# Reordering the pieces of a causal attention layer around its first and last tiles

## The chip, the cores and the metric

The kernel runs on one core of one Trainium2 chip. The metric is the device time of one execution in microseconds (us), lower is better; a number given for several runs is their median.

## The reference

An image of 256 channels and 64 x 64 positions goes through two layers in float32. Layer 0 is a convolution-like linear attention over windows, with its result added to the image. For layer 1 the image is 4096 tokens of 256 values; `t` below is the token matrix. It has two halves:

```
def causal(x):                      # x = layer norm of t, 4096 x 256
    q, k, v = x Wq + bq, x Wk + bk, x Wv + bv
    A = q k^T                       # 4096 x 4096, one head
    A = where(causal, A, MASK_FILL) / 16
    out = layernorm(softmax(A) v + x) * g_ln + beta_ln
    h = relu(out W1 + b1) W2 + b2
    return layernorm(h) * g_lnff + beta_lnff
t = t + causal(layernorm(t))
t = t + experts(layernorm(t))       # 2 of 8 experts, the same for all tokens
```

The routing of the experts needs the mean of the normalised tokens over all 4096 positions, so that no expert product can start before the last token has passed the causal half.

## The kernel before

`conv_attn_hybrid` builds one program of three stages: `window_attention` (layer 0), `causal_attention` and `experts`. This document is about `causal_attention`.

The 4096 tokens are 32 tiles of 128, in eight groups of four (group g holds tiles 4g to 4g + 3). A tile's scores are its queries against all keys up to its own position. Tiles 12 to 31 (`BIG` is 12) are called large, tiles 0 to 11 small. Large tiles are worked from 31 down to 12 in the list `larges`, small tiles from 0 up to 11 in `smalls`. One round of the main loop takes the large tile i and, as long as there are any, a small one.

The steps of a tile are these, with the names and lines that the profile shows:

- `queries(g)` (L950, L952): four matrix products of 512 columns for a group's queries, evicted by ScalarE (ACT) into `qT`.
- `scores(i)` gives a list of parts of 512 keys each. A part is two products into PSUM buffer `pa` (L991), an eviction by ACT into the row buffer `s` (large) or `ss` (small) (L993), for the first part a mask on GpSimd (POOL) (L996), and a maximum on VectorE (DVE) (L999). The last part also gives the row's maximum (L1002, L1003) and starts the exponential over the whole row on ACT (L1004).
- `attend(i)` gives a list of steps. `turn` transposes four blocks of 128 columns into PSUM buffer `pt` (L1021), and DVE copies them into `sT` (L1024, L1026 for the short block behind the row). `add` multiplies them with the values into `po` (L1035). The block behind the row carries the masked positions together; its product is with `after`. A step is the transposition of the next four blocks and then the products of these four. After the last step `finish` divides and takes statistics (L1045, L1047, L731, L732).
- `layers(g, j0, j1)` is what follows when a group's tiles are finished: six pieces `first` (normalise, L1075), `turn` (L1083, L1084), `hidden` (W1, L1092, L1094), `last` (W2 for four tiles, L1102, L1104, then L1109 and L1110), `norm` (L1117), `turn_again` (L1125 and L1126, whose result is the experts' input). The pieces wait in the list `later`; the main loop takes one at a time with `one()`. Group 3, the last to be finished, goes in two parts: tiles 1 to 3 of it when three are done, tile 0 at the end.
- `causal.values(g)` (L889, L891) gives four tiles of values.

PSUM buffers `pa`, `pt`, `po` and `pm` have two copies each, `sT` three. Only TensorE's (PE's) order is written out by hand, as the code calls it (`tc.manual_schedule`). The instructions of the other engines are placed by the framework's scheduler; each engine then works through its own list in order, and a wait at its head holds all behind it.

At the start of the stage, values and scores alternate: tile 31 is scored in eight parts, with `causal.values(6)`, `(5)` and `(4)` after the first three parts and `behind()` (which makes `after`) after the fifth. Small tile 0's queries and scores come in the first round.

Of the kernel before, what the change touches and what calls it, by code (L numbers as in the profile page):

```python
# [11 lines left out]
F32 = mybir.dt.float32  # L12
# [7 lines left out]
P = 128  # L20
# [707 lines left out]
def statistics(nc, pool, src, mv):  # L728

    st = pool.tile([P, 6], F32, name="lnst", bufs=4)  # L730
    nc.vector.bn_stats(out=st, in_=src)  # L731
    nc.vector.bn_aggr(out=mv, in_=st)  # L732


def rsqrt(nc, var, eps):
    nc.scalar.activation(var, var, AF.Sqrt, bias=eps)
    nc.vector.reciprocal(var, var)


BIG = NT - 20  # L740
# [184 lines left out]
def causal_attention(tc, t, ident, eps5, causal, big, given):  # L925
# [3 lines left out]
    nc = tc.nc  # L929
    with ExitStack() as ctx:  # L930
# [77 lines left out]
        def attend(i):  # L1008
# [5 lines left out]
            g = i // 4  # L1014
# [24 lines left out]
            def finish(acc):  # L1039
                if g not in atts:  # L1040
                    atts[g] = (sm.tile([P, 4, D], F32, name="att", bufs=3), sm.tile([P, 4, 2], F32, name="mvs", bufs=3), [])
                att, mvs, done = atts[g]
                xn = normalised(nc, sm, t[:, i, :], stats[:, i, 0:1], stats[:, i, 1:2], "xn", 2)
                l = sm.tile([P, 1], F32, name="l")
                nc.vector.reciprocal(l, acc[:, 0:1])  # L1045
                aj = att[:, i - 4 * g, :]
                nc.vector.scalar_tensor_tensor(aj, acc[:, 1:], l, xn, op0=ALU.mult, op1=ALU.add)  # L1047
                statistics(nc, sm, aj, mvs[:, i - 4 * g, :])
                done.append(i)
                if 4 * g != BIG:  # L1050
                    if len(done) == 4:
                        later.extend(layers(g, 0, 4))
                elif len(done) == 3:
                    later.extend(layers(g, 1, 4))
                elif len(done) == 4:
                    later.extend(layers(g, 0, 1))

            def step(at):
                if at + 1 < len(groups):
# [5 lines left out]
        def layers(g, j0, j1):  # L1065

            att, mvs, _ = atts[g]
            js, width, tail = range(j0, j1), (j1 - j0) * P, 4 * g == BIG
            state = {}

            def first():
# [21 lines left out]
                                         rhs=state["aT"][:, c, 0:width], start=(c == 0), stop=(c == DC - 1))  # L1093
                    nc.scalar.activation(hT[:, e, 0:width], pp[:, 0:width], AF.Relu, bias=col["b1"][:, e : e + 1])  # L1094

            def last():
                y, hT = att, state["hT"]
                mvy = sm.tile([P, 4, 2], F32, name="mvy")
                for j in js:
                    py = ps.tile([P, 512], F32, name="pm")  # L1100
                    for c in range(DC):
                        nc.tensor.matmul(py[:, 0:D], lhsT=hT[:, c, (j - j0) * P : (j - j0 + 1) * P], rhs=wt["W2"][:, c, :],  # L1102
                                         start=(c == 0), stop=(c == DC - 1))
                    nc.vector.tensor_add(y[:, j, :], py[:, 0:D], row["b2"])  # L1104
                    statistics(nc, sm, y[:, j, :], mvy[:, j, :])
                rsqrt(nc, mvy[:, j0:j1, 1], eps5)
                for j in js:
                    yj, tj = y[:, j, :], t[:, 4 * g + j, :]
                    nc.vector.scalar_tensor_tensor(yj, yj, mvy[:, j, 0:1], row["g_lnff"], op0=ALU.subtract, op1=ALU.mult)  # L1109
                    nc.vector.scalar_tensor_tensor(tj, yj, mvy[:, j, 1:2], tj, op0=ALU.mult, op1=ALU.add)  # L1110
                    statistics(nc, sm, tj, given.stats[:, 4 * g + j, :])

            def norm():
                rsqrt(nc, given.stats[:, 4 * g + j0 : 4 * g + j1, 1], eps5)
                for j in js:
                    s = given.stats[:, 4 * g + j, :]
                    nc.vector.tensor_scalar(att[:, j, :].rearrange("p (c q) -> p c q", c=DC),  # L1117
                                            t[:, 4 * g + j, :].rearrange("p (q c) -> p c q", c=DC),
                                            s[:, 0:1], s[:, 1:2], op0=ALU.subtract, op1=ALU.mult)
# [7 lines left out]
                                         accum_out=given.sums[:, c, given.parts : given.parts + 1])  # L1127
                given.parts += 1

            return [first, turn, hidden, last, norm, turn_again]  # L1130

        later = []
        with tc.manual_schedule(engines={mybir.EngineType.PE}):
# [9 lines left out]
            def one():  # L1143
                if later:
                    later.pop(0)()
# [1 line left out]
            causal.values(3, value_psum)  # L1147
            need(larges[0])
            causal.values(7, value_psum)
            for at, part in enumerate(scores(larges[0])):  # L1150
                part()
                if at < 3:
                    causal.values(6 - at, value_psum)
                if at == 4:
                    behind()
            for r, i in enumerate(larges):
                small = smalls.pop(0) if smalls else None
                if small is not None:
# [5 lines left out]
                if r + 1 < len(larges):  # L1164
# [4 lines left out]
                    one()  # L1169
                    todo.pop(0)()  # L1170
                    parts[-1]()
                if r == len(larges) - 1:
                    while todo:
                        todo.pop(0)()
                        one()
                half = len(todo) // 2
                for step in todo[:half]:
                    step()
                one()
                for step in todo[half:]:  # L1180
                    step()
                if small is not None:
                    for step in attend(small):
                        step()
                one()
            while later:
                one()
# [177 lines left out]
```

## Time and profile before

| | us |
|---|---|
| median of three runs | 1963.89 |
| lowest, highest | 1961.94, 1965.53 |
| the profiled execution's own time | 1963.31 |
| its span, first to last instruction | 1961.6 |
| mean granted TensorE clock | 0.988 of full |
| PE busy | 1867.7 (95%) |
| DVE busy | 1013.5 (52%) |
| ACT busy | 780.3 (40%) |
| POOL busy | 438.8 (22%) |

The causal stage lies between about 998 and 1717 us of the span; layer 0 lies before it, the routing from 1718 and the experts' products from 1730 to the end. In a row of the timeline the first number is the start in us from the span's start, the second the duration, and what stands in square brackets at the end is the idle time of the engine before this instruction and the instruction whose end released it.

### The profile page before, as it was taken

What the parts mean: (1) busy time and instruction counts of PE and PEld (TensorE: products, weight loads), DVE (VectorE), ACT (ScalarE), POOL (GpSimd) and SP (SyncE); (2) the same over time, 40 slices, a digit from 0 to 9 for tenths busy, and PEclk for the clock granted to TensorE, in tenths of its full rate; (3) what the DMA queues carried; (4) which work ended last, traced back from release to release, by engine and by line L of the source; (5) the groups of instructions that cost most, each with busy time, mean ns of one, the idle gap of its engine ahead of it and who ended that gap; (6) DMA issues with size and microseconds to landing.
All of it is one profiled execution on the core that took longest, in us unless ns stands there. A gap on an engine that the chain in (4) does not pass through costs nothing.

```text
span 1961.6 us, 50126 instructions
## 1 busy us (share of the span) xinstructions
PE 1867.7 (95%) x22286; PEld 1272.9 (65%) x22286; DVE 1013.5 (52%) x2154; ACT 780.3 (40%) x1295; POOL 438.8 (22%) x709
## 2 busy tenths in 40 slices
PE   3999999999999999999999999999999999789998
PEld 2666666666566667666665666665666666557777
DVE  4644555564654466666653435454554555543343
ACT  0566544444456645444413333233332333223322
POOL 1286233342255133432100000000000000031120
PEclk9999999999999999999999999999999999879999
DMA  8211100000331100002000000000000000010000
GB/s 246 75 56 41 40 14 14 19 19 13 112 88 37 49 19 19 13 13 51 13 2 1 0 1 0 1 1 1 0 1 0 1 1 1 1 43 22 22 22 22
DMA packets 66905, 53.58 MB, mean 27 GB/s; under 512 B 37568, under 2 KB 56792, under 8 KB 66688
## 3 DMA queue, kind: packets, MB, share of 16 engines
q1 hardware_dynamic: 57296, 31.87, 6.0%
q10 hardware_dynamic: 8128, 14.67, 2.1%
q0 software_dynamic: 1264, 3.84, 0.6%
q8 instruction: 174, 2.85, 0.6%
q14 instruction: 43, 0.35, 0.1%
HBM read 32.93 MB, written 17.44 MB: 26 GB/s over the span
## 4 chain that ended last, share of the span: by engine, by line
PE 43%; DVE 6%; ACT 3%; issue 1%; POOL 0%; ACTq 0%; DVEq 0%; POOLq 0%
PE po L1035 12%; PE pa L991 10%; PE ph L1299 6%; PE py L1319 6%; PE pt L1021 2%; PE pm L1092 1%; PE acc L395 1%; PE pm L1102 1%; PE ps L362 1%; PE ps L507 1%; DVE sT L1024 1%; DVE nbs L999 1%; DVE lnst L731 1%; PE pm L950 1%; ACT s L1004 1%
## 5 line engine op out<-in xcount | busy, mean ns | idle before, releaser
L330 ACT ACTIVATE pm<-ps 128x512 f32<-128x512 f32 (+24 forms) x690 | 358.4, 584 | 330.6 <-PE ps L362 176.8
L332 DVE TENSOR_SCALAR pm<-ps 128x512 f32<-128x512 f32 (+21 forms) x414 | 265.3, 668 | 265.2 <-PE ps L362 172.7
L362 PE MATMUL ps<-q,kh 32*128 32x217 f32 (+27 forms) x3872 | 213.1, 336 | 0.0
L395 PE MATMUL acc<-pm,vh 128*32 128x217 f32 (+27 forms) x3872 | 199.7, 329 | 0.0
L991 PE MATMUL pa<-k,qT 128*128 128x512 f32 (+3 forms) x416 | 180.2, 574 | 7.1 <-ACT qT L952 5.7
L362 PEld LDWEIGHTS ps<-q,kh 32*128 32x128 f32 x3872 | 161.2, 185 | 9.7
L1024 DVE COPY sT<-pt 128x512 f32<-128x512 f32 (+3 forms) x144 | 92.5, 642 | 143.1 <-PE pt L1021 142.9
L353 PE MATMUL ps<-table,table 32*128 32x184 bf16 (+36 forms) x2904 | 142.7, 245 | 5.4 <-issue 1.2
L395 PEld LDWEIGHTS acc<-pm,vh 128*32 128x32 f32 x3872 | 98.0, 109 | 71.7 <-issue 37.1
L430 POOL TENSOR_TENSOR y<-y,rn 128x512 f32<-128x512 f32 x32 | 40.9, 1277 | 432.8 <-DVE y L429 358.2
L993 ACT ACTIVATE s<-pa,v 128x512 f32<-128x512 f32 (+3 forms) x112 | 73.8, 661 | 152.2 <-PE pa L991 152.1
L991 PEld LDWEIGHTS pa<-k,qT 128*128 128x128 f32 x416 | 75.7, 191 | 89.3 <-issue 72.4
L353 PEld LDWEIGHTS <-table 32*128 32x128 bf16 x2904 | 57.0, 92 | 108.4 <-issue 97.6
L999 DVE TENSOR_REDUCE nbs<-s 128x1 f32<-128x512 f32 (+4 forms) x120 | 77.5, 651 | 80.6 <-ACT s L993 59.2
L1319 PE MATMUL py<-w,hT 128*128 128x256 f32 x512 | 111.8, 379 | 0.0
L1035 PE MATMUL po<-kh,sT 128*128 128x257 f32 x406 | 102.9, 395 | 8.7 <-DVE sT L1024 8.5
L1319 PEld LDWEIGHTS py<-w,hT 128*128 128x128 f32 x512 | 97.3, 190 | 15.7 <-issue 1.9
L362 PE MATMUL ps<-q,k 32*128 32x192 f32 (+30 forms) x1936 | 102.8, 337 | 0.0
L395 PE MATMUL acc<-pm,v 128*32 128x192 f32 (+30 forms) x1936 | 95.9, 326 | 0.6 <-issue 0.6
L507 PE MATMUL ps<-l0wo,y 128*128 128x256 f32 x384 | 90.7, 387 | 0.0
L1035 PEld LDWEIGHTS po<-kh,sT 128*128 128x128 f32 x406 | 74.7, 195 | 22.3 <-DVE sT L1024 12.7
L982 POOL MEMSET s<- 128x32 f32 x20 | 2.5, 124 | 376.5 <-PE pt L1021 348.4
(305 smaller groups left out, 2997.0 us busy)
## 6 DMA issues: line engine op xcount, KB each, us to landing
oscratch<-ov ACTq DMA_DIRECT2D x32, 256.0 KB
ov<-oscratch SPq DMA_DIRECT2D x32, 256.0 KB
t<-in_xT SPq DMA_DIRECT2D x32, 128.0 KB
vscratch<-v SPq DMA_DIRECT2D x32, 128.0 KB
vh<-vscratch SPq DMA_DIRECT2D x16, 256.0 KB
raw<-in_x ACTq DMA_DIRECT2D x7, 512.0 KB
raw<-in_x SPq DMA_DIRECT2D x7, 512.0 KB
out<-y SPq DMA_DIRECT2D x7, 512.0 KB
```

The source lines that it names most:

```text
L330: nc.scalar.activation(dst, src, AF.Relu)
L332: nc.vector.tensor_scalar_max(dst, src, 0.0)
L353: nc.tensor.matmul(got[h][:, spot].rearrange("p (y x) -> p y x", y=part.r1 - part.r0), lhsT=spread[hs, int(part.vertical), :], rhs=bias[hs ...
L362: nc.tensor.matmul(got[h][:, spot].rearrange("p (y x) -> p y x", y=part.r1 - part.r0), lhsT=keys[hs], rhs=q[hs, part.r0 : part.r1, part.c0 ...
L395: nc.tensor.matmul(out, lhsT=v, rhs=pm[:, h, spot].rearrange("p (y x) -> p y x", y=part.r1 - part.r0), start=fresh, stop=(left[key] == 0), ...
L507: nc.tensor.matmul(pt[:, i * D : (i + 1) * D], lhsT=ys[wi, Y][:, (2 * j + i) * P : (2 * j + i + 1) * P], rhs=wo[:, n, :], start=(n == 0), ...
L991: nc.tensor.matmul(pp[:, 0:m], lhsT=qTs[g][:, c, i * P - g * 512 : n - g * 512], rhs=x[b // 512][c][:, 0:m], start=(c == 0), stop=(c == DC ...
L999: nc.vector.tensor_reduce(nbs[:, at : at + 1], s[:, b : b + m], AX.X, ALU.max)
L1024: nc.vector.tensor_copy(sT[:, 0:full], pt[:, 0:full])
L1035: nc.tensor.matmul(acc, lhsT=sT[0:m, j * P : (j + 1) * P], rhs=rhs, start=(b == 0), stop=(m != P))
L1299: nc.tensor.matmul(ph, lhsT=w1v[:, e, c, f, :], rhs=x2[g][c], start=(c == 0), stop=(c == DC - 1))
L1319: nc.tensor.matmul(py, lhsT=hT[:, e, f, j * P : (j + 1) * P], rhs=w2v[:, e, f, :], start=(e + f == 0), stop=(e == 1 and f == FC - 1))
```

## The change

The change is in `layers`, in `finish` and in the main loop.

- At the start, the parts of tile 31's scores follow each other without values between them. After six of the eight parts come the queries and scores of small tile 0; then the last two parts, then the values of groups 4, 5 and 6, then small tile 0's attention. The small tiles thereby run one round ahead, and the round of tile 20 no longer has one.
- In a round, the small tile's first transposition is issued before the large tile's last step, and its other steps after it.
- A `layers` list of four tiles has nine pieces: `last` is two pieces of two tiles, and the scaling (L1109, L1110 and statistics) is a step `scale` of its own, also in two pieces. The square root of the last statistics moves from `norm` to the end of `scale`.
- `one()` is called at a third and two thirds of a large tile's steps, where it was called at the half.
- The last group goes as tiles 2 and 3, then tiles 0 and 1.

In the changed kernel the line numbers behind line 1053 differ: L1075, L1083, L1084, L1092, L1094, L1109, L1110, L1117, L1125, L1126 become L1073, L1081, L1082, L1090, L1092, L1113, L1114, L1122, L1130, L1131. The lines for queries, scores and attention, L1102 and L1104 stay. No computation is added or removed.

```diff
-                elif len(done) == 3:
-                    later.extend(layers(g, 1, 4))
-                elif len(done) == 4:
-                    later.extend(layers(g, 0, 1))
+                elif len(done) % 2 == 0:
+                    later.extend(layers(g, 4 - len(done), 6 - len(done)))
...
-            def last():
+            def last(sub):
                 y, hT = att, state["hT"]
-                mvy = sm.tile([P, 4, 2], F32, name="mvy")
-                for j in js:
+                if sub[0] == j0:
+                    state["mvy"] = sm.tile([P, 4, 2], F32, name="mvy")
+                mvy = state["mvy"]
+                for j in sub:
...
-                rsqrt(nc, mvy[:, j0:j1, 1], eps5)
-                for j in js:
+                if sub[-1] == j1 - 1:
+                    rsqrt(nc, mvy[:, j0:j1, 1], eps5)
+
+            def scale(sub):
+                y, mvy = att, state["mvy"]
+                for j in sub:
                     yj, tj = y[:, j, :], t[:, 4 * g + j, :]
                     nc.vector.scalar_tensor_tensor(yj, yj, mvy[:, j, 0:1], row["g_lnff"], op0=ALU.subtract, op1=ALU.mult)
                     nc.vector.scalar_tensor_tensor(tj, yj, mvy[:, j, 1:2], tj, op0=ALU.mult, op1=ALU.add)
                     statistics(nc, sm, tj, given.stats[:, 4 * g + j, :])
+                if sub[-1] == j1 - 1:
+                    rsqrt(nc, given.stats[:, 4 * g + j0 : 4 * g + j1, 1], eps5)
 
             def norm():
-                rsqrt(nc, given.stats[:, 4 * g + j0 : 4 * g + j1, 1], eps5)
...
-            return [first, turn, hidden, last, norm, turn_again]
+            subs = [(j, j + 1) for j in range(j0, j1, 2)]
+            return ([first, turn, hidden] + [lambda sub=sub: last(sub) for sub in subs]
+                    + [lambda sub=sub: scale(sub) for sub in subs] + [norm, turn_again])
...
-            for at, part in enumerate(scores(larges[0])):
-                part()
-                if at < 3:
-                    causal.values(6 - at, value_psum)
-                if at == 4:
+            for at, large in enumerate(scores(larges[0])):
+                large()
+                if at == 3:
                     behind()
+                if at == 5:
+                    need(smalls[0])
+                    first = smalls.pop(0)
+                    for part in scores(first):
+                        part()
+            for g in (4, 5, 6):
+                causal.values(g, value_psum)
+            for step in attend(first):
+                step()
...
-                if r == len(larges) - 1:
-                    while todo:
-                        todo.pop(0)()
+                behind_it = attend(small) if small is not None else []
+                pauses = range(len(todo)) if r == len(larges) - 1 else (len(todo) // 3, 2 * len(todo) // 3)
+                for at, step in enumerate(todo):
+                    if at == len(todo) - 1 and behind_it:
+                        behind_it.pop(0)()
+                    step()
+                    if at in pauses:
                         one()
-                half = len(todo) // 2
-                for step in todo[:half]:
+                for step in behind_it:
                     step()
-                one()
-                for step in todo[half:]:
-                    step()
-                if small is not None:
-                    for step in attend(small):
-                        step()
                 one()
```

## The prediction

> **What bounds the kernel now.** I read the page's first part first, then the chain, then the causal layer alone (about 1000 to 1718 us, all that the diff touches): its waits on PE, its stretches with the granted clock, and the timeline at each long wait.
>
> ```profile
> PE 1867.7 (95%) x22286; PEld 1272.9 (65%) x22286; DVE 1013.5 (52%) x2154; ACT 780.3 (40%) x1295; POOL 438.8 (22%) x709
> PE 43%; DVE 6%; ACT 3%; issue 1%; POOL 0%; ACTq 0%; DVEq 0%; POOLq 0%
> ```
>
> TensorE is the bound. The change adds no matrix work, so it can only give back time in which PE waits or runs at half clock. The waits of PE in the layer (total, times, longest):
>
> ```profile
> PE po L1035 <- DVE sT L1024: 8.5, 15, 1.5
> PE pt L1125 <- DVE att L1117: 7.5, 2, 4.0
> PE pa L991 <- ACT qT L952: 6.7, 6, 4.2
> PE pt L1021 <- ACT kh L1126: 3.8, 2, 2.1
> PE pt L1021 <- DVE aT L1084: 3.0, 5, 1.1
> PE pt L1083 <- DVE att L1075: 2.4, 1, 2.4
> PE po L1035 <- DVE sT L1026: 1.9, 2, 1.0
> PE pt L1021 <- ACT v L1126: 1.5, 3, 0.8
> ```
>
> Together 35 us. The true loss of a wait is some 0.16 us more than the idle shown: a transposition shows 0.27 us but back to back they start 0.11 apart. Now the stretches (columns: us, then busy PE, PEld, DVE, ACT, POOL, granted clock):
>
> ```profile
> 1035.95:1040.10 4.15, 0.00 (x0) 0.00 (x0) 0.00 (x0) 4.15 (x3) 0.00 (x0) 0.92 0.00 0
> 1040.10:1046.20 6.10, 6.10 (x11) 3.46 (x12) 1.21 (x4) 1.90 (x4) 0.58 (x2) 0.50 0.01 1
> 1226.00:1230.50 4.50, 2.78 (x14) 1.71 (x13) 3.98 (x17) 0.30 (x1) 0.22 (x2) 1.00 0.00 0
> 1230.60:1234.00 3.40, 3.40 (x9) 2.25 (x7) 1.42 (x5) 0.00 (x0) 0.64 (x1) 0.50 0.02 5
> 1686.00:1691.30 5.30, 5.17 (x16) 4.12 (x16) 2.01 (x3) 0.00 (x0) 0.00 (x0) 0.50 0.01 3
> 1702.05:1718.23 16.18, 7.09 (x23) 4.61 (x23) 10.09 (x36) 4.64 (x15) 1.51 (x3) 0.70 0.00 0
> ```
>
> Each longer hole is followed by a stretch at clock 0.50, which costs half its length again. The timeline says who held PE:
>
> ```profile
> 1035.74 3.73 ACT L1004 ACTIVATE s<-s,nb 128x4128 f32<-128x4128 f32 x1
> 1039.38 1.25 ACT L952 ACTIVATE qT<-pm,ik 128x512 f32<-128x512 f32 x2
> 1040.10 1.38 PE L991 MATMUL pa<-k,qT 128*128 128x128 f32 x4 [4.15 <-ACT qT L952]
> 1076.35 0.70 PE L1035 MATMUL po<-kh,sT 128*128 128x257 f32 x2 [0.61 <-DVE sT L1024]
> 1227.75 0.69 PE L1035 MATMUL po<-after,sT 32*128 32x257 f32 x2 [0.96 <-DVE sT L1026]
> 1656.71 2.01 PE L1035 MATMUL po<-kh,sT 128*128 128x257 f32 x8 [1.49 <-DVE sT L1024]
> ```
>
> **The change part by part.** Numbers are sums against the profiled execution's own 1963.31 us (span 1961.6 and 1.7 around it), 0.6 below the median of the three runs.
>
> *First exponentials under values.* Before, tile 31's exponential (table load 1.28 and 3.73 us) stands on ACT ahead of the evictions of the queries for small tile 0: PE idles 4.15 us, then 6.1 us at half clock lose 3.05. After, these queries and small 0's scores come before the last two score parts, and values 4, 5, 6 (12 tiles of 0.87 us, 10.4 us) follow, with small 0's attention. The large exponential ends some 6 us after the last part (eviction and reduction 0.69 each, 3.73, hops), under the 10.4. What comes in its place is the wait for a qT eviction as at the group boundary at 1189.49, 0.56 shown (0.7 in true loss); behind it on PE stand small 0's score and the two last parts, all now earlier than before. VectorE's value additions (0.42 each) keep PE's pace; three short waits on them, 0.2 to 0.5 us, stay about as they are. Gain 4.3 + 3.05 − 0.7 = 6.7.
>
> *Small transpositions ahead of the large tile's last step.* Twelve hand-overs between small transposition and product wait 0.35 to 0.76 us shown, 6.1 together, 8.0 in true loss. Small 0 keeps its own (0.77): nothing stands behind it. The cover of the others is the large tile's last step: zero to three products of 0.44 and one with `after` of 0.44. Needed are hop, copy (0.28 to 0.69) and hop, near 0.9. For tiles 31, 27 and 23 the last step has only the `after` product, so 0.2 to 0.4 stays; for tile 28 the second half of a `last` (L1104) comes just before, some 0.5 stays. Left over 2.0; gain 6.0. The change moves no DMA, and SP's queue keeps its order; POOL's memsets, masks and additions (0.1 to 0.64 each) move with the pieces and small scores by up to a round, on an engine that idles up to 30 us between them.
>
> *Layers in nine pieces.* The large `after` product at 1227.75 (and one at 1393.76, 0.97) stood behind a whole `last`: four L1104, four L1109, four L1110 and eight statistics, some 8 us of VectorE. In halves, and with the pieces that fall there (`first`, `turn`) behind other steps, these waits go: 1.9 + 0.3; with them the reason for the half clock at 1230.6 to 1234, 1.7. Gain 3.9. If the copies stay late, this is zero.
>
> The waits of transpositions for a pt buffer (3.0 on aT, 5.3 on L1126) depend on what a piece precedes. Counting pops (five a round with a small tile, four without): `turn` stands before another transposition only for tiles 20, 18, 15 and, with half width, 13; `turn_again` for tiles 27, 25, 23, 21 and 16, none of them just behind a large exponential. The others stand before scores. At 0.3 to 0.5 each, 3.5 of 8.3 stays: gain 4.8. In the late rounds (tiles 19 to 13) copies still queue behind layer steps on VectorE, as at 1656.71. Adding up that place again, from the start of the second half of `last`: VectorE has to the first copy's end two L1104 (0.84), five statistics and six aggregates (3.1), four L1109 (1.8), two L1110 (0.9), three score reductions (1.75), the tile's finish and small ones (1.2) and the copy (0.69), 10.3, of which 0.5 lies ahead: 9.8. PE has 1.74, scores of 0.87 and three of 1.72, and two turns, 8.6: a wait of 1.2 for 1.49. I count zero.
>
> *Table switches.* Sqrt and Exp alternate 14 times instead of 12: 28 loads for 24.
>
> ```profile
> L1004 ACT ACT_TABLE_LOAD x12 | 15.4, 1283 | 19.7 <-DVE nb L1003 19.7
> ```
>
> Four more are 5.1 us of ACT, of which the layer uses some 35%. The Trainium skill ("ScalarE: Activation LUTs", What ACT_TABLE_LOAD costs) speaks against it: a switch is 2.66 us, load and drain, so 10.6 us. In the trace the exponential at 1035.74 starts 0.02 after its load's end, and I take 1.28. They cost PE something only before an eviction it needs; such score waits are 0.2 to 0.6 before and about as many after: zero. Without the cover of two pa buffers, 5.1.
>
> *Last group by pairs.* Before, the last round (1682.17 to 1702.05) holds 14.3 us of products, 2.6 of waiting for L1075 and 3.0 of half clock; then 16.2 to the router's first product at 1718.23. After, the first pair's layer is over but for its scaling; the two rounds' products are 2 us fewer before the end of attention. But `turn_again` comes two steps (4.4 us) after `scale`, whose chain on VectorE (two L1109, two L1110, statistics, two Sqrt with hops, two L1117) takes some 7 with the copies in between: a new wait near 2.3. Behind it on PE stand tile 12's last transposition and its last six products, and everything after waits for those. So 0.2 to 3.6 us is gained there, by whether the clock falls. Behind it two tiles go through the chain: 0.4 more at each of five steps, 2 us more of products at half clock, less 2.5 for what the end before lost behind the first three tiles (L1110 to 1703.45, L1117, pt). Together −1.5 to +4.5; I take +1.
>
> The clock once more. The Trainium skill ("TensorE: Matmul & The Clock Gate", Part 1: The HAM clock gate) halves the clock after an idle window of about 3.4 us and restores it after a busy one. By that the first hole would cost 1.7, and the two of under 1 us at 1227 and 1230 none; the trace gave 3.05 and 1.7. By the rule the sum is 3 us less. I take the trace; for the end the rule speaks against pairs, and is in the sum.
>
> Sum: 6.7 + 6.0 + 3.9 + 4.8 + 1 = 22.4. I take 1.4 off for waits that lists of instructions do not show. 1963.3 − 21 = 1942.3; I say 1942.
>
> **The rivals.**
> *Half of it (1953 to 1948).* Hand-overs and buffers find the next wait: the hand-overs leave 4 instead of 2, pt waits stay at 6, the end is 3 worse, the clock falls once more. 22.4 − 2 − 2.5 − 4 − 2 = 12, so 1951. For it: VectorE is full in the late rounds; against it: the first two gains need no luck.
> *More (1934).* No half clock in the end (+3), and no new waits: 28.
> *Slower: copies behind the pieces.* 32 pieces (two `last`, two `scale` steps a group) are VectorE bursts of about 3 us, now in nearly every round. If each made a copy late as at 1656.71 (1.65 true), 53 us would be lost: 1994. It decides from 0.7 us a burst, where the 22.4 are used up. Against it: PE has 2.18 us a step, sT three buffers, and bursts of twice that length cost at most 0.96 before in early rounds.
> *It does not do it.* If `after`-only last steps were the rule, the hand-overs would stay; they are three of eleven. With the start hidden anyway: no, 4.15 us without any PE record are on the page.
>
> **How the numbers follow.** Forecast (gain 15 to 28) 0.66; half of it 0.22; more 0.06; about nothing 0.03; slower 0.03. What a measurement of this kernel can tell from no change is about 0.2%, 4 us. From the cases: faster 0.94, same 0.03, slower 0.03. The range, 1934 to 1952, leaves out gains under 12 and over 29.
>
> **What would show it.** No PE gap over 1 us and clock 1.00 from 1005 to 1060; one wait of 0.6 on qT there. PE's wait for sT from 8.5 to about 4, most of it in late rounds; L1026 near 0; the L1126 line's waits (after: L1131) under 3; no 0.50 near 1230; a wait of about 2 us for L1122 before the last tile ends; 28 table loads; attention's last product some 20 us earlier, and from there to the router's first product 15 to 18 us. It is wrong if the start keeps a hole, or if sT waits grow with the number of pieces.

## The result, and the profile after

The changed kernel takes 1939.95 us (median of 4 runs, 1937.32 to 1940.9); the kernel before, 1963.99 (4 runs, 1961.94 to 1965.53). The ratio is 0.9882, 95% interval 0.9870 to 0.9894: 23 us or 1.2% faster (24 us by the medians). The forecast was 1942 with a range of 1934 to 1952. The profiled execution after took 1937.32 us (span 1935.6); it is the fastest of the four, 2.6 us under their median. In it the causal layer, from the first queries' product on PE to the router's first product, lasts 691.15 us for 719.62 before; what follows the router's first product takes 243.1 for 243.4.

First part of the page and its chain, after:

```profile
PE 1855.2 (96%) x22286; PEld 1269.3 (66%) x22286; DVE 1016.5 (53%) x2154; ACT 785.5 (41%) x1299; POOL 439.4 (23%) x709
PE 47%; DVE 3%; ACT 2%; issue 1%; POOL 0%; ACTq 0%; DVEq 0%; POOLq 0%
```

The number of products is the same, so the gain is waiting and clock. On the chain DVE falls from 6% to 3%: copies and layer steps of VectorE that PE stood behind are beside its work now. The waits of PE in the causal layer (total us, times, longest), largest first:

```profile
PE pt L1130 <- DVE att L1122: 6.9, 2, 4.9
...
PE pa L991 <- ACT qT L952: 4.0, 5, 1.4
PE pa L991 <- ACT s L993: 3.9, 4, 1.3
...
PE pt L1081 <- DVE att L1073: 2.5, 1, 2.5
PE pt L1021 <- DVE aT L1082: 2.5, 4, 1.1
PE pt L1021 <- ACT kh L1131: 1.4, 3, 0.5
...
PE po L1035 <- DVE sT L1024: 1.2, 3, 0.5
PE pa L991 <- ACT ss L993: 1.0, 3, 0.3
```

Read it against the list of before, with this row, which the prediction does not show:

```profile
PE pa L991 <- ACT s L993: 1.3, 3, 0.6
```

sT has gone from 8.5 (15 times) to 1.2 (3), and its L1026 row (the `after` products) is missing; the hole of 4.2 on qT is gone. But the row `pa <- s` has gone from 1.3 to 3.9, and qT still has waits of up to 1.4. PE now waits for evictions of scores and queries by ScalarE more than before, and the forecast had counted that at zero.

The stretches (busy PE, PEld, DVE, ACT, POOL, then granted clock): the start, the place of the half clock near 1230, the last tile's wait, and the chain from attention's last product to the router.

```profile
1023.00:1040.50 17.50, 16.05 (x65) 11.35 (x63) 7.36 (x21) 7.66 (x7) 0.52 (x3) 1.00 0.01 1
1226.00:1234.00 8.00, 8.00 (x43) 6.14 (x42) 3.72 (x12) 0.00 (x0) 1.08 (x5) 1.00 0.01 2
1665.00:1676.90 11.90, 9.13 (x48) 7.07 (x47) 7.33 (x24) 1.43 (x6) 0.00 (x0) 1.00 0.00 1
1676.92:1692.52 15.60, 6.34 (x27) 3.85 (x25) 9.98 (x33) 3.50 (x10) 1.51 (x3) 0.89 0.00 0
```

No hole and full clock in the first two; in the third PE lacks 2.8 of 11.9 us, most of it the wait for L1122; the last stretch is 15.60 where before had 16.55:

```profile
1701.68:1718.23 16.55, 7.46 (x24) 4.61 (x23) 10.46 (x37) 4.64 (x15) 1.51 (x3) 0.70 0.00 0
```

Losses in true terms (start to start, less the time that such instructions take back to back), summed over the layer from the two traces, in us:

| what PE waits for | before | after |
|---|---|---|
| first hole on qT | 4.3 | 0.7 |
| other evictions by ScalarE (qT, s, ss) | 5.8 | 10.3 |
| sT: hand-overs of small tiles | 8.1 | 0.7 |
| sT: `after` products, large tiles' copies | 2.2 and 2.9 | 0 and 1.0 |
| pt buffers (aT, L1126 or L1131) | 11.3 | 6.7 |
| att (L1073 or L1075, L1117 or L1122) | 10.5 | 9.9 |
| excess with no releaser (half clock and small gaps) | 27.5 | 15.9 |

The rows make 27.4 of the 28.5 us between the two layers; the rest is not assigned. Most of the last row's 11.6 is half clock. In the layer before, the granted clock is 0.50 from 1039.4 to 1046.2, 1230.6 to 1234.0, 1684.6 to 1691.4, 1705.0 to 1711.9 and from 1715.3 on, with PE busy for 22.4 us of it; after, it is 0.50 only from 1689.0 on, with PE busy for 1.1. Two products of L1035 in a row start 0.43 us apart there and 0.22 at full clock, so about half of that busy time is lost: 11.2 and 0.6, an estimate.

### The profile page after: what moved, and what is told of

Its sections match the earlier page's. It is cut to its first block, busy times and chain, and to the rows that moved or that the text cites. A ratio compares the mean times of both kernels' runs of the same rounds, so it can differ in the third digit from the quotient of the medians.

```text
span 1935.6 us, 50137 instructions
## 1 busy us (share of the span) xinstructions
PE 1855.2 (96%) x22286; PEld 1269.3 (66%) x22286; DVE 1016.5 (53%) x2154; ACT 785.5 (41%) x1299; POOL 439.4 (23%) x709
## 4 chain that ended last, share of the span: by engine, by line
PE 47%; DVE 3%; ACT 2%; issue 1%; POOL 0%; ACTq 0%; DVEq 0%; POOLq 0%
PE po L1035 13%; PE pa L991 10%; PE ph L1310 6%; PE py L1330 6%; PE pt L1021 3%; PE pm L1090 1%; PE pm L1102 1%; PE pm L950 1%; PE acc L395 1%; PE ps L362 1%; PE ps L507 1%; PE po L889 1%; PE ps L889 1%; ACT L1004 0%; DVE nbs L999 0%
## 5 line engine op out<-in xcount | busy, mean ns | idle before, releaser
L991 PE MATMUL pa<-k,qT 128*128 128x512 f32 (+2 forms) x416 | 179.6, 572 | 5.6 <-ACT s L993 3.9
L1035 PE MATMUL po<-kh,sT 128*128 128x257 f32 x406 | 98.0, 381 | 1.2 <-DVE sT L1024 1.2
L507 PEld LDWEIGHTS ps<-l0wo,y 128*128 128x128 f32 x384 | 70.6, 190 | 22.9 <-POOL box L453 6.1
```

Source lines behind the costliest of these rows:

```text
L507: nc.tensor.matmul(pt[:, i * D : (i + 1) * D], lhsT=ys[wi, Y][:, (2 * j + i) * P : (2 * j + i + 1) * P], rhs=wo[:, n, :], start=(n == 0), ...
L991: nc.tensor.matmul(pp[:, 0:m], lhsT=qTs[g][:, c, i * P - g * 512 : n - g * 512], rhs=x[b // 512][c][:, 0:m], start=(c == 0), stop=(c == DC ...
L1035: nc.tensor.matmul(acc, lhsT=sT[0:m, j * P : (j + 1) * P], rhs=rhs, start=(b == 0), stop=(m != P))
```

## Experiments

All times were taken beside the kernel before on the same chip: 1963.09 for the first four kernels, 1963.32 for the next four, 1962.73 for the last four. Each ratio is to before; the changed kernel's is 0.9882. The changed kernel itself was not timed beside them, so "slower than the changed kernel" is said by the medians and by the ratios.

**The start alone, on the kernel before.** The new start, with the old hand-overs, six pieces, and three and one:

```diff
-            for at, part in enumerate(scores(larges[0])):
-                part()
-                if at < 3:
-                    causal.values(6 - at, value_psum)
...
+                if at == 5:
+                    need(smalls[0])
+                    first = smalls.pop(0)
...
+            for step in attend(first):
+                step()
```

> The kernel before with the new start alone: small tile 0's queries and scores stand before the last two score parts of tile 31, values 4, 5, 6 and small 0's attention behind them, so every small tile is one round earlier; the hand-overs, the six pieces and the 3 and 1 of the last group stay. Theory A (the change is a sum of places): the hole of 4.15 us and the 6.1 us at half clock behind it go, one wait of about 0.7 us on qT stays, 6.7 us gained: 0.9966 of before, about 1957. Theory B (the places are not independent: what the start frees is given back where the shifted small tiles meet the large ones' exponentials and layers): 0 to 3 us gained, 1961 to 1964, with PE waits on qT, s and pt longer than in before by what is missing.

Measured 1955.89, ratio 0.9965 (0.9952 to 0.9978), 7.2 us faster. Theory A. In its trace the start is as in the changed kernel:

```profile
1020.00:1037.50 17.50, 16.05 (x66) 11.43 (x64) 7.34 (x21) 7.66 (x7) 0.52 (x3) 1.00 0.01 1
```

Theory B has a part in it: four waits of 0.98 to 1.54 us true stand later in the layer, two each on s and on the second queries' qT, which before does not have in this form; all of PE's waits on evictions, the first qT wait left out, are 8.0 for 5.8. They came with the smalls being one round ahead: no table load was added here (24, as before).

**The start put back, in the changed kernel.** Values 6, 5, 4 behind the first three score parts, small tile 0 behind all eight:

```diff
+                if at < 3:
+                    causal.values(6 - at, value_psum)
...
-            for g in (4, 5, 6):
-                causal.values(g, value_psum)
-            for step in attend(first):
-                step()
+            need(smalls[0])
...
+                if r == 0:
+                    for step in attend(first):
+                        step()
```

> The changed kernel with the start put back: values 6, 5, 4 behind the first three score parts of tile 31, small tile 0's queries and scores behind all eight, its attention after the last score part of tile 30. Hand-overs, pieces, pairs and the smalls one round ahead stay. Theory A (the hole is what the start removes): a PE hole near 4 us on qT and about 6 us at clock 0.50 behind it come back, 6.5 to 7.5 us slower than the changed kernel, 1946 to 1947, the waits of the later rounds unchanged. Theory B (most of the start's worth lies in the smalls being one round ahead): 0 to 3 us slower, 1940 to 1943.

Measured 1944.05, ratio 0.9904 (0.9889 to 0.9920): 4 us slower than the changed kernel, between the theories. The trace has the hole and the half clock of theory A (0.72 over the 11 us behind the hole is 6.2 us at half):

```profile
1034.60:1038.80 4.20, 0.11 (x1) 0.00 (x0) 0.00 (x0) 4.20 (x3) 0.00 (x0) 0.95 0.00 0
1038.86:1050.00 11.14, 11.14 (x25) 6.34 (x26) 3.35 (x9) 4.17 (x8) 0.88 (x3) 0.72 0.00 1
```

The profiled layer is 8.7 us longer than the changed one's, the median only 4.1. Two numbers bring these closer. Late_ss below has the changed kernel's order and was timed on this run's chip: against it the median is 5.3 longer and the profiled layer 6.8 (699.88 for 693.04). And as wholes the two profiled executions (1942.06 and 1937.32) are only 4.7 apart, since layer 0, which is the same in both, took 4.0 longer in the changed kernel's. The start is worth 4 to 7.

**The hand-overs put back, in the changed kernel.** A step transposes the next four blocks and then multiplies the four that the step before transposed. So only at a tile's first products does nothing but two transpositions stand between a copy and the product that needs it, and there the change puts the large tile's last step.

```diff
-                    if at == len(todo) - 1 and behind_it:
-                        behind_it.pop(0)()
```

> The changed kernel with the small tiles' first transpositions put back behind the large tile's last step; all else as changed. Theory A: eleven waits of 0.5 to 0.75 us true loss between a small tile's transposition and its first product come back, about 7.3 us, less the 1.0 that the changed kernel still loses in two late rounds: 6 us slower than the changed kernel, about 1946, and sT L1024 back from 1.2 to 6 to 7 us shown. Theory B (the hand-over hides in waits that follow it anyway): only 2 to 3 us slower, 1942 to 1943.

Measured 1946.99, ratio 0.9913 (0.9899 to 0.9928): 7.0 us slower by the medians, 6 by the ratios. Theory A. The waits are back one by one, eleven of 0.51 to 0.85 true, 7.0 together:

```profile
PE po L1035 <- DVE sT L1024: 6.4, 14, 0.7
```

**Six pieces again, in the changed kernel.** The pauses change with the pieces (one at the half for two at the thirds), so this run does not tell the size of the pieces from their place.

```diff
-            return ([first, turn, hidden] + [lambda sub=sub: last(sub) for sub in subs]
-                    + [lambda sub=sub: scale(sub) for sub in subs] + [norm, turn_again])
+            def both():
+                for sub in subs:
+                    last(sub)
+                for sub in subs:
+                    scale(sub)
+
+            return [first, turn, hidden, both, norm, turn_again]
...
-                pauses = range(len(todo)) if r == len(larges) - 1 else (len(todo) // 3, 2 * len(todo) // 3)
+                pauses = range(len(todo)) if r == len(larges) - 1 else (len(todo) // 2 - 1,)
```

> The changed kernel with layers in six pieces again (both halves of the last products, then all of the scaling, in one piece) and two pauses a round as in the kernel before; start, hand-overs and pairs stay. Theory A: the waits of the large tile's product with after (0.96, 0.97 shown in before) and of transpositions for a pt buffer (8.3 shown in before, 5.9 true less after) come back, with the half clock near 1230: 6 to 9 us slower than the changed kernel, 1946 to 1949. Theory B (the hand-overs alone already moved those products off the bursts, and the pieces' position, not their size, sets the pt waits): 0 to 3 us slower, 1940 to 1943. Table loads on ScalarE: fewer than the 28 of the changed kernel would give some of the loss back on s and qT waits.

Measured 1948.60, ratio 0.9913 (0.9896 to 0.9930): 8.6 us slower by the medians, 6 by the ratios. The size is theory A's, the place is another. No wait on an `after` product came back, only one of 0.59 us true on the product just ahead of it, at both places (before had 1.12 and 1.13); nor did a half clock near 1230. What came are late copies of the large tiles themselves:

```profile
PE po L1035 <- DVE sT L1024: 6.8, 8, 1.8
...
PE pt L1021 <- ACT kh L1131: 2.9, 4, 1.7
```

The longest, on PE and then on VectorE (start, duration, in brackets the idle time and what ended it):

```profile
1575.20 0.60 PE L1021 MATMUL pt<-ident,s 128*128 128x128 f32 x4
1577.58 0.92 PE L1035 MATMUL po<-kh,sT 128*128 128x257 f32 x3 [1.77 <-DVE sT L1024]
```

```profile
1572.55 0.45 DVE L1114 SCALAR_TENSOR_TENSOR t<-att,mvy,t 128x256 f32<-128x256 f32 x1
1572.92 0.74 DVE L731 BATCH_NORM_STATS2 lnst<-t 128x6 f32<-128x256 f32 x2
...
1573.66 0.65 DVE L999 TENSOR_REDUCE nbs<-s 128x1 f32<-128x512 f32 x1
1574.23 0.17 DVE L732 BATCH_NORM_AGGREGATE stats<-lnst 128x2 f32<-128x6 f32 x1
1574.32 0.65 DVE L999 TENSOR_REDUCE nbs<-s 128x1 f32<-128x512 f32 x1
1574.89 0.17 DVE L737 RECIPROCAL stats<-stats 128x4 f32<-128x4 f32 x1
1574.98 0.65 DVE L999 TENSOR_REDUCE nbs<-s 128x1 f32<-128x512 f32 x1
1575.55 1.38 DVE L1122 TENSOR_SCALAR att<-t,stats 128x256 f32<-128x256 f32 x4
1576.84 0.68 DVE L1024 COPY sT<-pt 128x512 f32<-128x512 f32 x1
```

VectorE runs without a break: the whole scaling (L1114 and statistics), the score reductions that it had delayed, then L1122, and only then the copy that PE needs. Such waits are 0.96, 1.24, 1.94 and 1.65 us true, in rounds at 1427, 1526, 1576 and 1642; in the changed kernel nothing of a large tile waits over 0.51. Only the last of the four stands in the kernel before (1.65 at 1656.71); the other three come of six pieces in the new order. The profiled execution is the slowest of the six (1941.30 to 1951.38).

**Three tiles and one in the last group, in the changed kernel.**

```diff
-                elif len(done) % 2 == 0:
-                    later.extend(layers(g, 4 - len(done), 6 - len(done)))
+                elif len(done) == 3:
+                    later.extend(layers(g, 1, 4))
+                elif len(done) == 4:
+                    later.extend(layers(g, 0, 1))
...
-            subs = [(j, j + 1) for j in range(j0, j1, 2)]
+            subs = [tuple(range(j, min(j + 2, j1))) for j in range(j0, j1, 2)]
```

> The changed kernel with the last group's layer as three tiles and one again (tiles 15 to 13, then tile 12), still in pieces; start, hand-overs and pieces stay. Theory A (my term): pairs are worth 1 us at most either way plus what the clock does, so 1940 to 1942, with TensorE waiting 2 to 4 us for the first layer step of the three tiles. Theory B (the pairs keep the granted clock at 1.0 through the end chain, which before had 3 us of half clock): a stretch at 0.50 comes back before the last product of attention and the time is 3 to 5 us up, 1943 to 1945. Theory C (splitting costs at the end): 2 to 3 us faster, 1937, since only one tile passes through the chain of five steps behind attention.

Measured 1939.75, ratio 0.9877 (0.9862 to 0.9893): no difference from the changed kernel, theory A. Its profiled execution (1942.15, where the five lie between 1937.16 and 1942.20) looks like theory B, which the median does not bear out: the wait ahead of the last tile is 2.6 true (L1075) with the clock at 0.90 in the round, and the end takes 18.63 us at 0.66.

```profile
1663.00:1679.85 16.85, 15.12 (x63) 11.72 (x64) 7.86 (x22) 1.46 (x3) 0.00 (x0) 0.90 0.01 1
1679.85:1698.48 18.63, 7.58 (x24) 4.61 (x22) 11.44 (x41) 4.93 (x16) 1.50 (x3) 0.66 0.00 0
```

**The small exponential recorded later, in the changed kernel.** This was to test the new waits on s and qT: each small tile's exponential is recorded after the large tile's first transposition.

```diff
+                    exps[i] = lambda: nc.scalar.activation(s[:, 0 : n + NT], s[:, 0 : n + NT], AF.Exp, bias=nb, scale=1.0 / 16.0)
+                    if large or i == 0:
+                        exps[i]()
...
                     todo.pop(0)()
+                    if small is not None:
+                        exps[small]()
                     parts[-1]()
```

> The changed kernel with each small tile's exponential (with its table load, 1.28) recorded after the large tile's first transposition instead of at the end of the small scores; small 0's stays. It removes it from in front of the evictions of the large scores and of the second queries. Theory A (that exponential is what the waits on s, ss and the second qT are for: in the changed kernel 1.1, 1.5, 0.5, 1.5, 1.3, 1.3 us true loss, against 0.3 to 0.9 before): these go, 6 us faster than the changed kernel, about 1934; pa waits on s and ss under 1.5 in all. Theory B (the waits only move: the exponential is then late for the small transposition ahead of the last step, or the large one's exponential for the next round): within 2 us of the changed kernel, with new waits of pt on ss or s.

Measured 1938.77, ratio 0.9880 (0.9865 to 0.9895), as the changed kernel, and for a plain reason: the 1299 ScalarE and 2154 VectorE instructions of the trace stand in the same order as the changed kernel's. ScalarE's order isn't that of recording, so this edit tested neither theory. It gave instead a second profile of the same order, and that one is worth having. The last stretch in it:

```profile
1673.87:1691.34 17.47, 8.46 (x26) 5.49 (x24) 10.03 (x33) 3.53 (x10) 1.50 (x3) 0.75 0.00 0
```

The same instructions take 17.47 us at clock 0.75 here and 15.60 at 0.89 in the profile after. So 1.9 of the 28.5 us between the two profiled layers is the clock of one execution.

**Roots on GpSimd, in the changed kernel.** No Sqrt between the exponentials, so no loads between them:

```diff
+def root(nc, pool, var):
+    E, n = nc.gpsimd, var.shape[-1]
...
+    for _ in range(3):
+        E.tensor_mul(q, y, y)
+        E.tensor_mul(q, q, h)
+        E.tensor_scalar(q, q, 1.5, None, op0=ALU.add)
+        E.tensor_mul(y, y, q)
+    E.tensor_copy(var, y)
```

> The changed kernel with the reciprocal roots of the layers (all but those of the last pair) worked out on GpSimd (a guess in the integer pattern and three Newton steps, 16 small instructions) instead of Sqrt on ScalarE: no Sqrt lies between the exponentials, so the 28 table loads of the layer become 2 or 3, and 25 of 1.28 us leave ScalarE, 32 us. Theory A (loads in front of evictions cost PE about 5 us): the waits of pa on s and of the second queries on qT lose about 1 us each where the load stands in front, 4 to 6 us faster than the changed kernel, 1934 to 1936. Theory B (the exponential of the small tile itself, 0.85 to 1.6 us, is what stands in front, with or without a load): 1 to 2 us faster, 1938 to 1939. Against both: a GpSimd chain of 16 instructions takes longer than a Sqrt and can make a layer's step late; then att waits of transpositions (L1081, L1130 of the changed kernel) grow.

Measured 1989.05, ratio 1.0124 (1.0103 to 1.0146): 49 us slower than the changed kernel. Both theories fall, and the reservation was the main thing. The 16 instructions of a root start about 0.28 us apart, and from the first one's start to the last one's end it is 4.6 us. One root, as GpSimd, VectorE and ScalarE see it:

```profile
1285.02 0.22 POOL L744 TENSOR_SCALAR rh<-stats 128x4 f32<-128x4 f32 x1
...
1289.46 0.19 POOL L753 COPY stats<-ri 128x4 f32<-128x4 f32 x1
```

```profile
1289.69 0.41 DVE L1144 TENSOR_SCALAR att<-t,stats 128x256 f32<-128x256 f32 x1 [3.44 <-POOL stats L753]
1290.02 0.68 DVE L1015 TENSOR_REDUCE nbs<-ss 128x1 f32<-128x512 f32 x1
```

```profile
1291.58 1.17 ACT L1020 ACTIVATE ss<-ss,nb 128x1056 f32<-128x1056 f32 x1 [5.04 <-DVE nb L1019]
```

VectorE's next instruction in order needs the root, so VectorE stands 3.44 us; the small tile's reduction behind it is late, so its exponential is late on ScalarE, and the score evictions behind that come 3.5 us late for PE (10.4 us of waits on s in the layer, 20.7 on sT). Among these waits PE was busy at clock 0.50 for 34 us of the layer, for 1.1 in the changed kernel. Only the waits on the second queries are gone (qT 1.7 for 4.0), which speaks for theory A there.

**GpSimd roots and later recording together.**

> Both of these in the changed kernel: small exponentials recorded after the large tile's first transposition, and the layers' reciprocal roots on GpSimd. Theory A (loads and exponentials in front of evictions are the same loss, and one edit is enough): the same time as the better of the two within 1.5 us, about 1934. Theory B (each takes away its own part): 3 us below the better one, about 1931.

Measured 1988.27, ratio 1.0128 (1.0112 to 1.0143): the same as with the roots alone, since later recording again moved little. It tells nothing more.

**One table for the layer, in the changed kernel.** Roots as exp(-0.5 ln(x)) on ScalarE, and one load of a table with both functions ahead of the first exponential:

```diff
+def rsqrt_ln(nc, var, eps):
+    nc.scalar.activation(var, var, AF.Ln, bias=eps)
+    nc.scalar.activation(var, var, AF.Exp, scale=-0.5)
...
+                    if not loaded:
+                        loaded.append(tc.keep_in_program_order(nc.add_instruction(mybir.InstLoadActFuncSet(
+                            act_func_set_id=6, name=nc.get_next_instruction_name(), engine=mybir.EngineType.Activation))))
...
-                rsqrt(nc, mvs[:, j0:j1, 1], eps5)
+                rsqrt_ln(nc, mvs[:, j0:j1, 1], eps5)
```

(and so for the other two roots of a layer.)

> The changed kernel with the layers' reciprocal roots as exp(-0.5 ln(x)) on ScalarE, and one table load ahead of the causal layer of a table that holds both Exp and Ln: 27 of the 28 loads of the layer go (35 us of ScalarE), each root is two small ScalarE instructions instead of one and a reciprocal on VectorE; nothing that VectorE or GpSimd does is added, which is where the GpSimd roots of no_switch went wrong. Theory A (the step that failed in the prediction is the switches counted at zero: loads ahead of evictions cost PE about 5 us): waits of pa on s (3.9 shown) and of the second queries on qT (2.6 of 4.0 shown) fall to under 2.5 together, 4 to 6 us faster than the changed kernel, 1934 to 1936. Theory B (the small tile's exponential itself, 0.85 to 1.6 us, stands ahead of those evictions; the load before it is a minor part): 1 to 2 us faster, 1938.

Measured 1927.89, ratio 0.9824 (0.9804 to 0.9844): 12 us faster than the changed kernel by the medians, 11 by the ratios. Theory A, and more than it said. The edit does a second thing: the reciprocals leave VectorE and with them a hop between the engines. No run has that alone; late_two below, which keeps the roots as they were, shows that the waits on s and qT go without it. PE's waits on evictions are down to the three first ones of query groups and three short ones; there is no row for s:

```profile
PE pa L996 <- ACT qT L957: 1.7, 3, 0.6
...
PE pa L996 <- ACT ss L998: 1.0, 3, 0.3
```

From the two traces, true losses: 7.2 us on s and the second qT go, 0.7 on aT, 0.5 on sT and 0.8 on L1130 (L1122 of the changed kernel), 9.2 in all, and against the second profile of the changed order the layer is 9.9 us shorter (683.16 for 693.04).

**The same in the kernel before.**

> The kernel before with the same roots: 23 of its 24 loads go. Theory A (in the kernel before, evictions lose only about 3 us true to all of pa's waits on s and ss, half of it behind a load): 1 to 3 us faster than before, 1961 to 1962, so the change is worth 26 to 27 us without switches and 24 with them. Theory B (loads cost both kernels the same): 4 to 6 us faster, 1958 to 1960, and the change is worth the same 24 us.

Measured 1953.24, ratio 0.9956 (0.9938 to 0.9973): 9.5 us faster by the medians, 8.6 by the ratio.

```profile
PE po L1043 <- DVE sT L1032: 9.6, 14, 2.3
...
PE pa L996 <- ACT qT L957: 5.1, 5, 3.0
```

Theory A falls: the same edit is worth nearly as much before as after, only elsewhere. In its trace the first hole is 3.13 us true instead of 4.31, a load of 1.28 shorter; the waits on s (2.1) are gone; and the three longest waits for a pt buffer on L1126 (2.30, 0.98, 1.87 us true in before) are down to 0.5 each; two late copies of large tiles wait 1.7 longer in exchange. Not all of it is loads: the half clock near 1230 is gone as well, and of the 11.7 us by which the profiled layer is shorter about 3 are half clock (PE busy at 0.50 for 16.1 us, for 22.4 in before). Without switches the change is 1953.24 to 1927.89, by the ratios 1.3%; with them 1.2%. So the switches take some 1 to 3 us from this change, inside the intervals.

**Small exponentials tied behind the large evictions, in the changed kernel.** As late_ss, but the exponential is bound to come after the eviction of the large tile's last score part but one:

```diff
+                        with tc.issue_after(evicted[larges[r + 1]].ins):
+                            exps[small]()
```

> The changed kernel with each small tile's exponential (small 0's excepted) tied behind the eviction of the large tile's last score part but one in ScalarE's order; in late_ss it was only recorded later, and ScalarE's order stayed as it was. Table loads as in the changed kernel. Theory A (exponential and load in front of evictions are what the waits on s and the second qT are for): 1.1 and 1.5 on qT and 0.5 to 1.5 on s go, 5 to 6 us faster, about 1934. Theory B (the waits only move, to the last part's eviction, the large exponential or the small transposition): within 2 us of the changed kernel, with waits of pt on ss or larger ones of sT.

Measured 1929.57, ratio 0.9833 (0.9813 to 0.9853): 10 us faster than the changed kernel. Theory A, in place and sign, and nearly twice its size; the 28 loads are all still there. The row of s is gone, and of qT only the first waits of query groups are left:

```profile
PE pa L991 <- ACT qT L952: 1.7, 3, 0.6
```

The place where the changed kernel had its longest wait on s, in the changed kernel and then here (ScalarE):

```profile
1281.55 1.28 ACT L1004 ACT_TABLE_LOAD   x1 [1.72 <-DVE nb L1003]
...
1282.85 1.17 ACT L1004 ACTIVATE ss<-ss,nb 128x1056 f32<-128x1056 f32 x1
1283.93 1.25 ACT L993 ACTIVATE s<-pa,v 128x512 f32<-128x512 f32 x2
...
1284.65 1.13 PE L991 MATMUL pa<-k,qT 128*128 128x512 f32 x2 [1.32 <-ACT s L993]
```

```profile
1283.99 0.69 ACT L993 ACTIVATE s<-pa,v 128x512 f32<-128x512 f32 x1 [1.03 <-PE pa L991]
1285.71 0.69 ACT L993 ACTIVATE s<-pa,v 128x512 f32<-128x512 f32 x1 [1.03 <-PE pa L991]
...
1287.57 1.28 ACT L1004 ACT_TABLE_LOAD   x1
1288.86 1.18 ACT L1004 ACTIVATE ss<-ss,nb 128x1056 f32<-128x1056 f32 x1
```

In the changed kernel, load and exponential, 2.5 us, stand ahead of two evictions, and both pa buffers are full before they end. Here they stand behind, and the evictions wait for PE instead of PE for them. In one_set the same exponential stands ahead of the evictions without its load, 1.2 us, and PE waits for nothing: here two buffers cover the one and not the two.

**Both.**

> Both: one table for the layer, and small exponentials behind the large tile's evictions. Theory A (one loss, either edit takes it): within 1.5 us of the better of the two. Theory B (each takes its own part): 2 to 3 us below it, about 1932. It is the candidate for a kernel better than both.

Measured 1927.51, ratio 0.9828 (0.9809 to 0.9847). Theory A: one loss, and either edit takes it. One_set, late_two and one_late are not told apart by these runs; each is faster than both kernels of the case.

## Why the prediction was right or wrong

The forecast's case was gains of 15 to 28 us; 23 came. By its own steps:

- *First exponentials under values, 6.7.* Right where it looked: the hole and the half clock behind it are gone, the one qT wait is 0.72 us true, as said, and the clock is 1.00. Alone the start gives 7.2, taken out it costs 4 to 5. What the step left out is that smalls one round ahead put their exponentials before other evictions: 2.2 us, seen in start_only. It took account of the start only.
- *Small transpositions, 6.0.* Right, a little small: 7.0 when undone (6 by the ratios), 7.4 in the table. The 2.0 allowed for short last steps was too much; only small tile 0 keeps its 0.66, and tiles 31, 27, 23 and 28 do not wait.
- *Nine pieces, 3.9 and 4.8.* The size was right (6 to 9 when undone), the mechanism only in part. The waits for pt buffers went from 11.3 to 6.7, near the 4.8, but six pieces bring back less than 2 of that. The two `after` waits are gone, but of their 2.2 six pieces with the hand-overs bring back 1.2, so the hand-overs (or the pops they shift) take the rest. The half clock near 1230, 1.7 of the 3.9, stays away with six pieces too. The step that failed is "I count zero" for the late rounds: with bursts of `last` and `scale` in one piece the copies of large tiles wait 0.96 to 1.94 us four times, with small pieces not over 0.51. Adding up VectorE's queue at one place of the old kernel gave 1.2 for 1.49 and hid that the place itself moves with the burst.
- *Table switches, zero.* The step that failed against the change. The count of 28 loads is right:

```profile
L1004 ACT ACT_TABLE_LOAD x14 | 18.0, 1283 | 17.5 <-DVE nb L1003 17.4
```

  (as many before Sqrt). PE's waits on evictions grew from 5.8 to 10.3 us true, 4.5, close to the 5.1 that was kept as the cost "without the cover of two pa buffers". The two buffers are no cover for a load and an exponential in one. But it is the place and not the number of loads: start_only adds no load and has half of the growth, late_two keeps all loads and has none of it. The Trainium skill ("ScalarE: Activation LUTs", What ACT_TABLE_LOAD costs) gives 2.66 us for a switch; here 1.283 us of load is followed by the exponential after 0.02 us. By the page four switches are 10.6 us of ScalarE, an estimate, and by the trace 5.1; neither count is what PE loses.
- *Last group by pairs, +1.* Right in size: nothing that can be measured. The new wait for L1122 was put near 2.3 and is 2.15 us true; attention's last product stands 24.8 us earlier for "some 20", and from there the router is 15.6 us away (17.5 in the second profile) for 15 to 18. The half clock that the step feared inside the last round did not come in the profile; that it comes elsewhere at the end is a matter of the execution.
- *Sum.* 22.4 less 1.4 for 23 is closer than its terms, and that is luck in part. 4.5 lost to evictions was not in it. Nor was, with the other sign, 1.9 on late copies of large tiles, 1.4 on the hand-overs and much of the clock: by the table's estimate half clock fell by 10.6 us, where the forecast had 4.75 firm and up to 3 more in the last group. In the second profile of the changed order PE is busy at 0.50 for 6.2 us, so there the fall is 8.1.

Of the rivals, copies behind pieces turned over: the pieces are what keeps copies from being late. "Half of it" had the right reason (a new wait elsewhere), but named pt and sT and not ScalarE's evictions.

What stays open: how much of the fall in half clock repeats from run to run, and what the smalls one round ahead are worth by themselves (no_cover keeps them there). Undone one at a time, start, hand-overs, pieces and pairs make 20 us by the medians and 16 by the ratios, of 24 and 23; with intervals of some 3 us each, that does not show a part that is missing.

## What to carry to other kernels

When work is moved a round ahead, list what each of its instructions now stands in front of on a shared engine: here an exponential with its table load came before evictions that TensorE needs, and tying it behind them gave 10 us. A burst on an engine that works in order may be better cut into pieces: here the same scaling delayed copies by up to 1.94 us in one piece and by 0.51 at most in small ones. Look for functions that share a table before counting switches as free: one load in place of 28, with the roots it needs, was worth 11 us here, and one in place of 24 was worth 9 in the kernel before.

## What was not expected of the hardware

- *The half clock is partly chance.* One order of instructions ended in 15.60 us at clock 0.89 and in 17.47 at 0.75. And in layer 0, which the change does not touch, the profile after is at half clock where before is not (before, then after):

```profile
505.00:510.00 5.00, 4.51 (x11) 1.81 (x10) 3.85 (x12) 1.20 (x2) 0.89 (x2) 1.00 0.46 187
505.00:510.00 5.00, 4.23 (x5) 1.85 (x6) 4.68 (x14) 0.60 (x1) 0.00 (x0) 0.50 0.20 79
```

  The causal layer of after starts 2.75 us later; this stretch and a shorter one near 95 us lie ahead of it. So the half clock of before near 1230 need not come of its place either. It stands behind waits of 0.96 and 0.76 us (1.12 and 0.92 in true loss). At the same place start_only has two waits, 0.86 and 0.76 shown, that end at 1192.6 and 1195.5, and the stretch behind the first is at full clock:

```profile
1194.30:1202.00 7.70, 6.94 (x32) 4.66 (x31) 6.16 (x20) 1.42 (x4) 1.87 (x5) 1.00 0.00 0
```

  The whole stretches of half clock in before's layer last 6.8 or 3.4 us: 6.8 behind the hole of 4.15, 3.4 behind these two waits of under 1. Whether the 0.10 us between 0.96 and 0.86 matters was not tested. Single executions of one kernel differ by several us (1941.30 to 1951.38 in six, not all of it clock), so a clock term of 1.7 to 3 us in a forecast is a mean over executions and not a certain gain.
- *A small GpSimd instruction on 128 x 4 elements takes 0.19 to 0.23 us and mostly starts 0.28 us after the last one,* so a root in 16 of them is 4.6 us with what lies between, where Sqrt and reciprocal are 0.29 and 0.17.
